# Rotary halves exchanged by DMA, rotation spread over two steps, and routing pieces re-placed in a two-layer attention and expert kernel

## The chip, the cores and the metric

The kernel runs on one core of one Trainium2 chip. The metric is device time of one launch in microseconds (us), as the median of the runs shown. A profile is one further execution, recorded by the hardware profiler; its times are only compared with its own.

The core has five engines which run side by side and meet through semaphores: TensorE (PE in the profile; PEld is its weight load), VectorE (DVE), ScalarE (ACT), GpSimd (POOL) and SyncE (SP), which here only issues DMAs.

## The reference

Input `x` is 16 sequences of 256 tokens with 128 features. Two layers follow each other. A layer normalises `x` and adds an attention and a feed-forward part, both of the normalised `x`. Only the first layer's attention and routing are touched by the change:

```
xn = layernorm(layernorm(x)) * ln_g + ln_b
qk, v = split(xn @ w_qkv.T)                      # queries and keys are the same projection, 8 heads of 64
q = qk*cosq + rotate_half(qk)*sinq               # rotate_half: (x1, x2) -> (-x2, x1), halves of 32
k = qk*cosk + rotate_half(qk)*sink
attn = softmax(q @ k.T, masked to a local window)
out = (attn @ v) @ w_out.T
router: softmax over 8 experts of layernorm(x), the best 2 per token
expert part: gelu MLP of 256 hidden units per expert, weighted; plus one shared MLP
```

The second layer is a gated attention unit and a 32-expert feed-forward part, in which all experts are computed for all tokens. All arithmetic is in float32.

## The kernel before, in words

**Tiling.** The 4096 tokens are eight groups `g` of 512 tokens, two sequences each, laid out with 128 on the partitions. Heads go in pairs, since two heads of 64 fill 128 partitions. So there are 32 head pairs `n = 4*g + hp`; each holds two sequences, and one sequence of one head pair is one *step* `s` of the attention loop: 64 steps, two for each `n`.

**Stages.** The first stage (L485 to L556) runs attention and routing of layer one. The second (L574 on) computes the shared MLP of layer one and then 39 tiles of 256 tokens through their expert. The third (L648 on) gathers the results back and computes layer two.

**What one step does.** The loop `for s in range(-3, NS + 1)` (L500) is a software pipeline written out by hand: `manual_schedule` (L469) keeps the program's order on PE, DVE, ACT and POOL. SP is not in that list. In step `s`:

- PE transposes the probabilities of step `s` (`turned0`, L429, 8 matmuls), computes the scores of step `s+3` (`scores`, L395, 8 matmuls) and the output of step `s-1` (`attended`, L446, 8 matmuls).
- ACT empties the transposes (`evicted`, L436), takes the exponentials of step `s+2` (L411) and copies the output (L451).
- DVE masks the scores of step `s+3` and finds the row maxima (L401), and divides the probabilities of step `s+1` by their sums (`divided`, L417 and L420).

PE's transposes of step `s+1` need the divisions that DVE makes in step `s`.

**The rotation.** `rotated(n)` (L361) is called at the end of every odd step. PE makes two projections, `pq` with `wqk` (L366) and `pw` with `wqks` (L368), whose columns are those of `wqk` with the halves of 32 exchanged. In the next, even, step DVE makes four products (`products`, L377: `pq*cosq`, `pq*cosk`, `pw*sinq`, `pw*sink`) ahead of the scores and of the division, and then two sums (`sums`, L381): that of `q` runs on POOL, that of `k` on DVE after the division. Before the loop the first of these is made at once (L484 to L487).

**Routing.** `routed(g)` (L321) is a generator of eight pieces: moments of the rows (L143 to L149), normalisation (L155 to L166), a transpose, the router's matmuls (L216), the logits, the exponential, the ranking (`before`, five operations of 256 elements on DVE, L200 to L209), and its end. A piece of group `g` runs in step `6*(g-2)+d` for `d` in `(0, 3, 5, 6, 7, 8, 9, 10)` (L477 to L480). `prepare(g)` makes the attention's own input; `values(g, c)` the values (L353).

**Places.** From step 40 on `places0` (L234) works out the row of each token in the list sorted by expert. Its third piece, in step 42, contains the DVE's last partial sums (`ex`, L256) and the PE matmuls over them (L258 to L261). `scatter0(n)` (L308) then writes 128 rows twice by indirect DMA from POOL, in steps 45 to 62. Before that `x_rows` is filled with zeros by one large DMA on SP (L551), in step 10.

Of the kernel before, what the change touches and what calls it, by code (L numbers as in the profile page):

```python
# [11 lines left out]
F32 = mybir.dt.float32  # L12
# [7 lines left out]
P = 128  # L20
# [27 lines left out]
def two_layers(ctx: ExitStack, tc: tile.TileContext, a: dict, out: bass.AP):  # L48
# [17 lines left out]
    def mm_tile(name):  # L66
        tags, n = turn
        turn[1] += 1
        return bank(tags[n % len(tags)], name)
# [4 lines left out]
    def load(name, shape, src=None, eng=None, pool=const):  # L74
        t = pool.tile(shape, F32, tag=name, name=name)
        (eng or nc.scalar).dma_start(out=t, in_=a[name] if src is None else src)
        return t
# [10 lines left out]
    w_a = first.enter_context(tc.tile_pool(name="w_a", bufs=1))  # L88
    wv = load("wv", [P, 512], pool=w_a)
    wqk = load("wqk", [P, 512], pool=w_a)  # L90
    wqks = load("wqks", [P, 512], pool=w_a)
    cosq = load("cosq", [P, N], pool=w_a, eng=nc.sync)
    sinq = load("sinq", [P, N], pool=w_a, eng=nc.sync)
    cosk = load("cosk", [P, N], pool=w_a, eng=nc.sync)
# [141 lines left out]
    def places0(wk):  # L236

        nch = NG * NC
        fl = lambda t: t.rearrange("p n e -> p (n e)")
        top, sel = (wk.tile([P, nch, E0], F32, tag=f"m{i}", name=f"m{i}", bufs=1) for i in range(2))  # L240
        nc.vector.tensor_scalar(fl(sel), fl(rk_all), 2.0, None, ALU.is_lt)
        nc.vector.tensor_scalar(fl(top), fl(rk_all), 0.0, None, ALU.is_equal)
        nc.vector.tensor_tensor(fl(w0_all), fl(sel), fl(pr_all), ALU.mult)
        yield

        acc = sel
        for i in range(5):
            k = 1 << i
            nxt = wk.tile([P, nch, E0], F32, tag=f"cum{i % 2}", name=f"cum{i}", bufs=1)
            nc.vector.tensor_copy(nxt[:, :k, :], acc[:, :k, :])  # L250
            nc.vector.tensor_tensor(nxt[:, k:, :], acc[:, k:, :], acc[:, : nch - k, :], ALU.add)
            acc = nxt
            if i == 2:
                yield
        ex = wk.tile([P, nch, E0], F32, tag="ex", name="ex", bufs=1)
        nc.vector.tensor_tensor(ex, acc, sel, ALU.subtract)  # L256
        pos_ps = mm_tile("pos_ps")[:, : nch * E0]
        nc.tensor.matmul(pos_ps, upper, fl(sel), start=True, stop=False)  # L258
        nc.tensor.matmul(pos_ps, ones, fl(ex), start=False, stop=True)
        cnt = mm_tile("cnt_ps")[:, :E0]  # L260
        nc.tensor.matmul(cnt, ones, acc[:, nch - 1, :], start=True, stop=True)  # L261
        yield
        ns = T // RT
        full = wk.tile([P, E0, ns], F32, tag="full", name="full", bufs=1)
        nc.vector.tensor_tensor(
            full, cnt.unsqueeze(2).to_broadcast([P, E0, ns]), steps.unsqueeze(1).to_broadcast([P, E0, ns]), ALU.is_gt
        )
        used = wk.tile([P, E0], F32, tag="used", name="used", bufs=1)
        nc.vector.tensor_reduce(used, full, AX.X, ALU.add)
        low = wk.tile([P, E0, E0], F32, tag="low", name="low", bufs=1)  # L270
        nc.vector.tensor_tensor(
            low, used.unsqueeze(1).to_broadcast([P, E0, E0]), tie0.rearrange("p (i j) -> p i j", j=E0), ALU.mult
        )
        begin = wk.tile([P, E0], F32, tag="begin", name="begin", bufs=1)
        nc.vector.tensor_reduce(begin, low, AX.X, ALU.add)
        row0 = wk.tile([P, E0], F32, tag="row0", name="row0", bufs=1)
        nc.vector.tensor_scalar(row0, begin, float(RT), None, ALU.mult)
        pos = wk.tile([P, nch, E0], F32, tag="pos", name="pos", bufs=1)
        nc.vector.tensor_tensor(
            pos, pos_ps.rearrange("p (n e) -> p n e", e=E0), row0.unsqueeze(1).to_broadcast([P, nch, E0]), ALU.add  # L280
        )
        yield
        nc.vector.tensor_tensor(fl(sel), fl(sel), fl(top), ALU.subtract)
        for s, m in enumerate((top, sel)):
            at = wk.tile([P, nch, E0], F32, tag="at", name=f"at{s}", bufs=1)
            nc.vector.tensor_tensor(at, m, pos, ALU.mult)
            atr = wk.tile([P, nch], F32, tag="atr", name=f"atr{s}", bufs=1)
            nc.vector.tensor_reduce(atr, at, AX.X, ALU.add)
            nc.vector.tensor_copy(slot_at[:, s, :], atr)
        yield  # L290
        for s, m in enumerate((top, sel)):
            nc.vector.tensor_tensor(m, m, pr_all, ALU.mult)
            nc.vector.tensor_reduce(slot_w[:, s, :], m, AX.X, ALU.add)
        yield

        le = wk.tile([P, NT0, E0], F32, tag="le", name="le", bufs=1)
        nc.vector.tensor_tensor(
            le, begin.unsqueeze(1).to_broadcast([P, NT0, E0]), tiles.unsqueeze(2).to_broadcast([P, NT0, E0]), ALU.is_le
        )
        ex_t = wk.tile([P, NT0], F32, tag="ex_t", name="ex_t", bufs=1)  # L300
        nc.vector.tensor_reduce(ex_t, le, AX.X, ALU.add)
        nc.vector.tensor_scalar(ex_t, ex_t, -1.0, None, ALU.add)
        off = wk.tile([P, NT0], F32, tag="off", name="off", bufs=1)
        nc.vector.tensor_scalar(off, ex_t, float(P), None, ALU.mult)
        nc.vector.tensor_copy(tile_off, off)
        yield
# [15 lines left out]
    with first as pa:  # L322
# [33 lines left out]
        def over(t):  # L356
            return t.unsqueeze(1).to_broadcast([P, 2, N])
# [3 lines left out]
        def rotated(n):  # L361

            g, hp = divmod(n, 4)
            h = slice(hp * P, (hp + 1) * P)
            pq = mm_tile(f"pq_{g}_{hp}")
            nc.tensor.matmul(pq, wqk[:, h], xhTs0[g], start=True, stop=True)  # L366
            pw = mm_tile(f"pw_{g}_{hp}")
            nc.tensor.matmul(pw, wqks[:, h], xhTs0[g], start=True, stop=True)  # L368
            heads[n] = got = [
                wk.tile([P, 2, N], F32, tag=f"rot{what}", name=f"{what}_{g}_{hp}", bufs=3) for what in "qk"  # L370
            ]
            parts = [wk.tile([P, 2, N], F32, tag="rots", name=f"s{what}_{g}_{hp}", bufs=3) for what in "qk"]

            def products():
                for to, ps_, by in ((got, pq, (cosq, cosk)), (parts, pw, (sinq, sink))):
                    for t, m in zip(to, by):
                        nc.vector.tensor_tensor(t, ps_.rearrange("p (b n) -> p b n", n=N), over(m), ALU.mult)  # L377

            def sums():
                for r, part, eng in zip(got, parts, (nc.gpsimd, nc.vector)):  # L380
                    eng.tensor_tensor(r, r, part, ALU.add)  # L381

            turning.append((products, sums))


        def scores(s):
# [78 lines left out]
        with tc.manual_schedule(engines={order.PE, order.DVE, order.Activation, order.Pool}):  # L465
# [13 lines left out]

            pieces = {}  # L480
            for g in range(1, NG):
                for d in (0, 3, 5, 6, 7, 8, 9, 10):
                    pieces.setdefault(6 * (g - 2) + d, []).append(g)

            step(routing, 0, 2)  # L485
            step(preparing, 0, 2)
            rotated(0)  # L487
            products, sums = turning.pop()
            products()
            sums()  # L490
            step(routing, 0, 2)
            step(routing, 1, 2)
            step(preparing, 1)
# [3 lines left out]
            step(routing, 0, 2)  # L497
            step(routing, 1)
            rotated(1)
            for s in range(-3, NS + 1):  # L500
                g, r = divmod(s, 8)
                if 0 <= s < NS:
# [3 lines left out]
                    pTs[s] = evicted(s, tps)  # L506
                if 0 <= s + 2 < NS:
                    sms[s + 2] = exponentials(s + 2, *sc[s + 2])
                products, sums = turning.pop() if turning else (None, None)
                if products:  # L510
                    products()
                    if s + 3 < NS:
                        sc[s + 3] = scores(s + 3)
                    if 0 <= s + 1 < NS:
                        divided(s + 1, sc[s + 1][0], sms.pop(s + 1))
                    sums()
                else:
                    if 0 <= s + 1 < NS:
                        divided(s + 1, sc[s + 1][0], sms.pop(s + 1))
                    if s + 3 < NS:  # L520
                        sc[s + 3] = scores(s + 3)

                if s in (-2, -1):
                    step(routing, 0)
# [5 lines left out]
                    step(preparing, g + 2)  # L530
                if s == 40:
                    placing = places0(wk)
                if 40 <= s < 47:
                    next(placing)
                if s >= 1:
                    attended(s - 1, pTs.pop(s - 1))

                if s % 2 and 2 <= (s + 5) // 2 < NS // 2:
                    rotated((s + 5) // 2)
                if s < 0:  # L540
                    continue
                if r == 2 and g:
# [4 lines left out]
                if s == 10:  # L547
# [1 line left out]
                    nc.gpsimd.memset(zero, 0.0)  # L549
                    x_r0 = x_rows.rearrange("(t p c) d -> p t (c d)", p=P, c=2)  # L550
                    nc.sync.dma_start(out=x_r0, in_=zero.unsqueeze(1).to_broadcast([P, NT0, 2 * D]))  # L551
                if 45 <= s < 63:
                    for n in range((s - 45) * 16 // 9, (s - 44) * 16 // 9):
                        scatter0(n)
            project(NG - 1)
    turn[0] = ["mm", "s", "mm", "o", "mm", "s"]  # L556
# [357 lines left out]
def _laid_out(v):  # L914
# [1 line left out]
    d["x"] = v["L0_attn_x"].reshape(T, D)  # L916
    qk, vv = v["L0_attn_w_qkv"][:512], v["L0_attn_w_qkv"][512:]
    d["wqk"] = qk.T
    d["wqks"] = qk.reshape(HEADS, 2, 32, D)[:, ::-1].reshape(512, D).T
    d["wv"] = vv.T  # L920
    d["wo"] = v["L0_attn_w_out"].T.reshape(4, P, D).transpose(1, 0, 2)
    d["rtw"] = v["L0_ffn_router_w"]
# [57 lines left out]
```

## Time and profile before

| | us |
|---|---|
| three runs | 1104.29, 1105.55, 1106.56 |
| median | 1105.55 |
| profiled execution | 1138.63 |
| its span, first to last instruction | 1136.6 |
| start, up to the output copy of step 0 | 0 to 51.5 |
| copies of steps 0 to 39 (with routing) | 51.5 to 272.5 |
| copies of steps 39 to 45 (with places) | 272.5 to 314.5 |
| copies of steps 45 to 57 (with scatters) | 314.5 to 397.0 |
| copies of steps 57 to 63 | 397.0 to 431.5 |
| second and third stage | 431.5 to 1136.6 |

The stage borders are starts of the copies of the attention output (L451), of which each step has one. In a line of the profile, `out<-in` are tile names of the program, `x128` counts instructions, and the time after `<-` is idle time that ended with the named releaser. The duration of a DVE instruction includes its latency: four divisions of about 350 ns each follow each other every 260 ns, and products of 680 ns every 600 ns. Where several follow on one engine, the spacing is the cost.

### The profile page before, as it was taken

The page shows a single profiled execution, that of the slowest core. Times are in us where ns is not written, and L with a number is a line of the kernel's source. Part 1 is how long each engine was busy: PE and PEld are TensorE (multiplying, and loading weights), DVE is VectorE, ACT ScalarE, POOL GpSimd, SP SyncE. Part 2 cuts the span into 40 slices and gives each one's busy share as a digit, 9 for nine tenths or more (in the row PEclk, how much of TensorE's full clock was granted, in tenths as well). Part 3 has the DMA queues.
Part 4 walks back from the last instruction along what each step waited for, and adds up shares of the span by engine and source line. Part 5 has one row for each costly group of instructions (what it writes and reads, how often), then busy time and mean ns, then how long its engine had stood idle before and what let it go on. Part 6 is the DMA issues. An engine that isn't in the chain of part 4 may idle for free.

```text
span 1136.6 us, 13298 instructions
## 1 busy us (share of the span) xinstructions
PE 983.9 (87%) x3976; PEld 551.0 (48%) x3976; DVE 737.4 (65%) x2346; ACT 442.9 (39%) x1096; POOL 266.0 (23%) x241
## 2 busy tenths in 40 slices
PE   4899899999878859999458797989979699899998
PEld 1455555555444424599433443445444354445453
DVE  3999888989686721233345556667665676758663
ACT  1566666666454643344121222222322223223221
POOL 2111111111156650000243206041240502403020
PEclk9899999999899869999768898999989999899999
DMA  5004100000011115399304242322323323242330
GB/s 157 1 1 142 40 1 1 1 2 1 5 33 38 36 39 164 114 268 265 94 21 116 53 102 56 83 70 73 78 72 84 74 61 83 57 104 56 77 84 9
DMA packets 68471, 80.00 MB, mean 70 GB/s; under 512 B 7976, under 2 KB 43568, under 8 KB 68016
## 3 DMA queue, kind: packets, MB, share of 16 engines
q1 hardware_dynamic: 61984, 69.20, 22.5%
q0 software_dynamic: 4096, 8.40, 2.6%
q10 hardware_dynamic: 2320, 1.56, 0.4%
q8 instruction: 32, 0.52, 0.2%
q14 instruction: 39, 0.32, 0.1%
HBM read 62.09 MB, written 17.04 MB: 70 GB/s over the span
## 4 chain that ended last, share of the span: by engine, by line
PE 62%; DVE 19%; issue 7%; POOL 6%; another core or an unknown queue 2%; DMA 1%; ACT 1%; POOLq 0%; ACTq 0%; DVEq 0%
PE u L853 8%; PE g L851 8%; PE z L862 7%; DVE p L401 4%; PE s L395 4%; POOL yg L668 3%; PE t L429 3%; PE yr L636 3%; PE o L446 3%; PE h L626 3%; DVE p L420 3%; PE o L814 2%; PE pq L366 2%; PE y L457 2%
## 5 line engine op out<-in xcount | busy, mean ns | idle before, releaser
L855 ACT ACTIVATE h<-g 128x512 f32<-128x512 f32 x128 | 76.4, 597 | 268.0 <-PE g L851 267.9
L856 DVE TENSOR_TENSOR h<-h,u 128x512 f32<-128x512 f32 x128 | 87.4, 683 | 82.5 <-PE u L853 81.4
L853 PE MATMUL u<-xn1Ts,eu 128*128 128x512 f32 x256 | 134.6, 614 | 0.0
L851 PE MATMUL g<-xn1Ts,eg 128*128 128x512 f32 x256 | 134.3, 607 | 0.0
L411 ACT ACTIVATE p<-p,nm 128x256 f32<-128x256 f32 x256 | 127.1, 506 | 2.5 <-DVE nm L401 2.5
L401 DVE CUSTOM_DVE_ANT_0 p<-s,mask 128x256 f32<-128x256 f32 x256 | 93.1, 419 | 41.7 <-PE s L395 21.5
L862 PE MATMUL z<-h,ed 128*128 128x512 f32 x224 | 117.5, 607 | 0.0
L668 POOL DMA_INDIRECT yg<-y_rows,slot_at x64 | 67.8, 1059 | 188.5 <-issue 156.1
L429 PE MATMUL t<-ident,p 128*128 128x128 f32 x512 | 74.7, 290 | 33.6 <-DVE p L420 30.0
L436 ACT COPY pT<-t 128x512 f32<-128x512 f32 x128 | 69.4, 589 | 86.1 <-PE t L429 68.0
L789 POOL TENSOR_TENSOR r1s<-r1s,sinr 128x512 f32<-128x512 f32 x16 | 23.2, 1453 | 326.8 <-DVE r1s L787 326.8
L429 PEld LDWEIGHTS t<-ident,p 128*128 128x128 f32 x512 | 62.7, 148 | 70.7 <-issue 44.0
L858 DVE TENSOR_TENSOR h<-h,bc 128x512 f32<-128x512 f32 x128 | 90.8, 710 | 3.0
L395 PE MATMUL s<-k,q 64*128 64x256 f32 x512 | 83.0, 435 | 3.0 <-DVE nm L401 1.1
L446 PE MATMUL o<-pT,v 128*64 128x256 f32 x512 | 74.4, 414 | 11.0 <-ACT oT L451 6.0
L381 POOL TENSOR_TENSOR q<-q,sq 128x512 f32<-128x512 f32 x32 | 40.7, 1272 | 182.2 <-DVE sq L377 182.2
L420 DVE TENSOR_SCALAR p<-p,sm 128x256 f32<-128x256 f32 x256 | 75.9, 359 | 2.3
L853 PEld LDWEIGHTS u<-xn1Ts,eu 128*128 128x128 f32 x256 | 49.5, 198 | 56.9 <-issue 51.2
L851 PEld LDWEIGHTS g<-xn1Ts,eg 128*128 128x128 f32 x256 | 48.0, 196 | 44.2 <-issue 37.7
L862 PEld LDWEIGHTS z<-h,ed 128*128 128x128 f32 x224 | 43.4, 197 | 52.1 <-issue 44.5
L311 POOL DMA_INDIRECT x_rows<-xn_all,slot_at x64 | 62.7, 980 | 22.2 <-issue 17.9
L176 PE MATMUL xn1T<-ident,xn 128*128 128x128 f32 x32 | 10.5, 436 | 61.4 <-DVE xn L155 61.4
(256 smaller groups left out, 1607.6 us busy)
## 6 DMA issues: line engine op xcount, KB each, us to landing
bc<-rows_r SPq DMA_DIRECT2D x128, 256.0 KB, 4.0
we<-in_ex_dram SPq DMA_DIRECT2D x39, 257.0 KB, 4.0
x_rows<-zero SPq DMA_DIRECT2D x1, 4992.0 KB, 16.7
xt<-x_rows SPq DMA_DIRECT2D x39, 128.0 KB, 3.9
y_rows<-yt SPq DMA_DIRECT2D x39, 128.0 KB, 3.5
x<-in_x_dram SPq DMA_DIRECT2D x8, 256.0 KB, 4.6
out_dram<-out SPq DMA_DIRECT2D x8, 256.0 KB, 2.3
x_rows<-xn_all,slot_at POOLq DMA_INDIRECT x64
```

Of the source, the lines that this page charges most:

```text
L395: nc.tensor.matmul(sp[h][:, i, :], q[rows, b, i * P : (i + 1) * P], k[rows, b, :], start=True, stop=True)
L401: nc.vector.tensor_tensor_reduce(out=pr[:, h, i, :], in0=sp[h][:, i, :], in1=mask[:, i, :], scale=-1.0, scalar=-NEG, op0=ALU.add, op1=ALU. ...
L411: nc.scalar.activation(row, row, AF.Exp, bias=nm[:, n : n + 1], scale=-1.0, accum_out=sm[:, n : n + 1])
L420: nc.vector.tensor_scalar(row, row, sm[:, n : n + 1], None, ALU.mult)
L429: nc.tensor.transpose(tp[:, at : at + P], pr[:, h, i, j * P : (j + 1) * P], ident)
L446: nc.tensor.matmul(op[h * DH : (h + 1) * DH, :], vs[g][:, 2 * b + j, (2 * hp + h) * DH : (2 * hp + h + 1) * DH], pT[:, h, j, :], start=(j ...
L668: nc.gpsimd.indirect_dma_start(out=yg[:, 2 * c + s, :], out_offset=None, in_=y_rows, in_offset=bass.IndirectOffsetOnAxis(ap=slot_at[:, s, ...
L851: nc.tensor.matmul(gp, wg, xnT, start=True, stop=True)
L853: nc.tensor.matmul(up, wu, xnT, start=True, stop=True)
L856: nc.vector.tensor_tensor(h, h, up, ALU.mult)
L858: nc.vector.tensor_tensor(h, h, wT[n // 2][:, n % 2, :], ALU.mult)
L862: nc.tensor.matmul(zp, w, r, start=(n == 1), stop=False)
```

## The change

- `wqks` and the projection `pw` are gone. ACT copies `pq` to SBUF (`here`), and four DMAs on SP write it to `there` with each block of 32 partitions exchanged with its neighbour (`q ^ 32`). The copy stands in `later`, so that ACT makes it ahead of its evictions in the next step.
- The rotation takes two steps: `near` (the two cosine products, from PSUM) in the even step, `far` (the two sine products, from `there`) in the odd one after it, followed by both sums on POOL. `rotated` is called one step pair earlier, `(s+7)//2` in place of `(s+5)//2`.
- `divided` comes before `scores` in every step; `near` before both, `far` between them.
- The normalisation of a group moves from `d=3` to `d=2`.
- `places0` has one more `yield`, between `ex` and the matmuls over it. The scatters run in steps 46 to 61, two `n` in each, in place of 45 to 62.

```diff
-    wqks = load("wqks", [P, 512], pool=w_a)
...
         nc.vector.tensor_tensor(ex, acc, sel, ALU.subtract)
+        yield
         pos_ps = mm_tile("pos_ps")[:, : nch * E0]
...
-            pw = mm_tile(f"pw_{g}_{hp}")
-            nc.tensor.matmul(pw, wqks[:, h], xhTs0[g], start=True, stop=True)
             heads[n] = got = [
                 wk.tile([P, 2, N], F32, tag=f"rot{what}", name=f"{what}_{g}_{hp}", bufs=3) for what in "qk"
             ]
-            parts = [wk.tile([P, 2, N], F32, tag="rots", name=f"s{what}_{g}_{hp}", bufs=3) for what in "qk"]
-
-            def products():
-                for to, ps_, by in ((got, pq, (cosq, cosk)), (parts, pw, (sinq, sink))):
-                    for t, m in zip(to, by):
-                        nc.vector.tensor_tensor(t, ps_.rearrange("p (b n) -> p b n", n=N), over(m), ALU.mult)
+            parts = [wk.tile([P, 2, N], F32, tag=f"rots{what}", name=f"s{what}_{g}_{hp}") for what in "qk"]
+            here = wk.tile([P, 2, N], F32, tag="here", name=f"here_{g}_{hp}")
+            there = wk.tile([P, 2, N], F32, tag="there", name=f"there_{g}_{hp}")
+
+            def copied():
+
+                nc.scalar.copy(here.rearrange("p b n -> p (b n)"), pq)
+                for q in range(0, P, 32):
+                    to = q ^ 32
+                    nc.sync.dma_start(out=there[to : to + 32], in_=here[q : q + 32])
+
+            def near():
+                for t, m in zip(got, (cosq, cosk)):
+                    nc.vector.tensor_tensor(t, pq.rearrange("p (b n) -> p b n", n=N), over(m), ALU.mult)
+
+            def far():
+                for t, m in zip(parts, (sinq, sink)):
+                    nc.vector.tensor_tensor(t, there, over(m), ALU.mult)
 
             def sums():
-                for r, part, eng in zip(got, parts, (nc.gpsimd, nc.vector)):
-                    eng.tensor_tensor(r, r, part, ALU.add)
+                for r, part in zip(got, parts):
+                    nc.gpsimd.tensor_tensor(r, r, part, ALU.add)
 
-            turning.append((products, sums))
+            later.append(copied)
+            turning.append([near, far, sums])
...
-                for d in (0, 3, 5, 6, 7, 8, 9, 10):
+                for d in (0, 2, 5, 6, 7, 8, 9, 10):
                     pieces.setdefault(6 * (g - 2) + d, []).append(g)
...
             rotated(0)
-            products, sums = turning.pop()
-            products()
-            sums()
+            drain(later)
+            drain(turning.pop())
...
             rotated(1)
+            drain(later)
+            turning[0].pop(0)()
             for s in range(-3, NS + 1):
...
-                products, sums = turning.pop() if turning else (None, None)
-                if products:
-                    products()
-                    if s + 3 < NS:
-                        sc[s + 3] = scores(s + 3)
-                    if 0 <= s + 1 < NS:
-                        divided(s + 1, sc[s + 1][0], sms.pop(s + 1))
+                if turning and len(turning[0]) == 3:
+                    turning[0].pop(0)()
+                    far = sums = None
+                else:
+                    far, sums = turning.pop(0) if turning else (None, None)
+                if 0 <= s + 1 < NS:
+                    divided(s + 1, sc[s + 1][0], sms.pop(s + 1))
+                if far:
+                    far()
+                if s + 3 < NS:
+                    sc[s + 3] = scores(s + 3)
+                if sums:
                     sums()
-                else:
-                    if 0 <= s + 1 < NS:
-                        divided(s + 1, sc[s + 1][0], sms.pop(s + 1))
-                    if s + 3 < NS:
-                        sc[s + 3] = scores(s + 3)
...
-                if 40 <= s < 47:
+                if 40 <= s < 48:
                     next(placing)
...
-                if s % 2 and 2 <= (s + 5) // 2 < NS // 2:
-                    rotated((s + 5) // 2)
+                if s % 2 and 2 <= (s + 7) // 2 < NS // 2:
+                    rotated((s + 7) // 2)
...
-                if 45 <= s < 63:
-                    for n in range((s - 45) * 16 // 9, (s - 44) * 16 // 9):
+                if 46 <= s < 62:
+                    for n in range(2 * (s - 46), 2 * (s - 45)):
                         scatter0(n)
```

More of the change, by code (lines that the diff above doesn't have):

```diff
@@ L918, in _laid_out @@
     d["wqk"] = qk.T
-    d["wqks"] = qk.reshape(HEADS, 2, 32, D)[:, ::-1].reshape(512, D).T
     d["wv"] = vv.T
```

## The prediction

> **What bounds the kernel now.** First the page, for span and engine shares; second the five stretches of the first stage, since a share over the whole span says nothing of the stage that the change touches; third the waits inside the longest stretch; fourth single durations and the order in time of one stalled step.
>
> ```profile
> span 1136.6 us, 13298 instructions
> ...
> PE 983.9 (87%) x3976; PEld 551.0 (48%) x3976; DVE 737.4 (65%) x2346; ACT 442.9 (39%) x1096; POOL 266.0 (23%) x241
> ```
>
> In the table of stretches the columns are length, PE, PEld, DVE, ACT and POOL busy, granted clock, DMA share and GB/s:
>
> ```profile
> 30.40:51.50 21.10, 18.02 (x82) 10.91 (x81) 20.18 (x83) 11.19 (x39) 3.76 (x3) 0.76 0.01 2
> 51.50:272.50 221.00, 206.48 (x1180) 120.61 (x1180) 200.18 (x777) 150.10 (x471) 36.76 (x32) 0.98 0.07 24
> 272.50:314.50 42.00, 35.72 (x175) 20.16 (x176) 32.11 (x122) 21.72 (x71) 5.48 (x5) 0.88 0.01 4
> 314.50:397.00 82.50, 68.22 (x344) 38.74 (x343) 59.41 (x212) 44.56 (x141) 53.62 (x53) 0.92 0.12 37
> 397.00:431.90 34.90, 21.00 (x112) 11.79 (x111) 8.79 (x37) 14.41 (x44) 15.77 (x17) 0.71 0.10 32
> ```
>
> While routing runs (51.5 to 272.5, 39 steps, 5.67 us each) PE is busy for 93% and DVE for 91%: two engines bound it together, and each now and then waits for the other:
>
> ```profile
> PE t L429 <- DVE p L420: 12.7, 8, 4.0
> DVE p L401 <- PE s L395: 9.0, 15, 1.7
> ```
>
> The eight PE waits come where a step's DVE queue is long: normalisation and ranking both fall in step 6k+3, and the four products of step 6k+4 follow before the division that PE's transposes need. The intervals between output copies show it: 8.92, 9.25, 7.90 and 7.86 us before the copies of steps 16, 22, 28 and 34, among others of 3.6 to 7.1. Step 42 holds the longest wait; PE waits for the partial sums, and then DVE for PE:
>
> ```profile
> 288.10 1.22 PE L259 MATMUL pos_ps<-ex,ones 128*128 128x256 f32 x2 [4.08 <-DVE ex L256]
> ...
> 298.00 0.42 DVE L401 CUSTOM_DVE_ANT_0 p<-s,mask 128x256 f32<-128x256 f32 x1 [8.69 <-PE s L395]
> ```
>
> From step 45 on neither is full (68.2 and 59.4 of 82.5); PE waits 12.3 us there for the division that comes after products and masks.
>
> **What the Trainium skill says.** "DMA: Bandwidth & Descriptors", in the anatomy of one DMA, gives a fixed 2.0 us and bytes over 436 GB/s; for 64 KB that is an estimate of 2.15 us. The trace is near: a 64 KB store from SBUF takes 1.6 us, 64 KB loads 2.2 to 2.6. The same page, on queues, rings and completion order, has descriptors consumed in ring order: a small DMA waits behind a large one of its queue. "SBUF — State Buffer", on the two separate sides, says that a DVE operation with two SBUF inputs and a GpSimd operation that reads SBUF lock each other out for a whole instruction. The trace agrees in the one place where they meet: the first `k` sum, begun while POOL adds `q`, takes 1264 ns instead of 683. "GPSIMD Engine Reference", on elementwise work, has an add on GpSimd 1.96 times as long as on DVE; here it is 1.86:
>
> ```profile
> L381 POOL TENSOR_TENSOR q<-q,sq x32: 1264/1271/1282, 21.4 to 393.4; 128x512 f32<-128x512 f32 x32
> L381 DVE TENSOR_TENSOR k<-k,sk x32: 676/683/1264, 22.0 to 396.8; 128x512 f32<-128x512 f32 x32
> ```
>
> **The change part by part.** *Six steps with routing (three pairs).* Spacings from the order in time on DVE: masks of one step 1.37 us, reciprocal and four divisions 1.26, a product or a sum 0.60. Two steps cost 2 x 2.63 + 4 x 0.60 + 0.60 = 8.26, so six 24.8. One group's routing adds moments 1.3, normalisation 1.5, logits 0.55, ranking 2.7, and `xh` 0.8 x 6/8: together 31.4. The change takes one sum of 0.60 from each pair: 29.6. PE: transposes 0.87, scores 1.06, outputs 1.01 in each step, `pq` and `pw` 1.91 in each pair, and per group values 3.8, projection 3.6, input transpose 0.6 (each x 6/8), router and its transpose 1.6: 17.6 + 5.7 + 6.0 + 1.6 = 31.0, at clock 0.98 31.6; without `pw` 28.1, or 28.7. Before, six steps took 34.0, so the fuller engine was busy for 31.6/34.0 = 0.93. After, DVE is the fuller. I add 0.6 for the port lock: ranking and logits, with two SBUF inputs, follow `far` and its sums in odd steps, and one such meeting costs 1.264 - 0.683 = 0.58. So 30.2/0.93 = 32.5, 1.5 less per six steps, 9.8 us over 39. On top comes what the new order removes of the 12.7 us of PE waits: division ahead of masks, two products in a step instead of four, normalisation away from ranking. I take a third, 4.2. Its bounds are nothing and all. Together **14 us**.
>
> *Exchange.* ACT gains 0.59 us (its 128x512 eviction) in every even step; it is busy for 68% of that stretch and stood idle 48.4 us before its evictions, for the transposes, just where the copy now stands. So it costs nothing; without that cover it would cost 0.59 x 30 = 18 us. On SP nothing but the zero fill stands between 15 and 435 us. Queued issues there follow each other every 0.48 us. The trace has no SBUF-to-SBUF transfer; the nearest rows give
>
> ```profile
> rows_r<-wT SPq DMA_DIRECT2D x8, 64.0 KB, 1.6
> uvs<-in_uvs_dram SPq DMA_DIRECT2D x1, 64.0 KB, 2.6
> ```
>
> and I take 2.2, bounds 1.6 and 4.0 (the usual landing of the 128 to 256 KB rows). The last quarter lands 0.59 + 3 x 0.48 + 2.2 = 4.2 us after `pq` is done. Meanwhile DVE has `near`, a division, masks and the next division before `far`: 1.20 + 1.26 + 1.37 + 1.26 = 5.1 in the lightest steps, 6.9 on average steps. So `far` does not wait; behind it are the masks of its step, for which ACT's exponentials wait.
>
> *Start.* Nothing covers the exchange of `n = 0` and `n = 1`. DVE had `pq` at 19.2 and ended the first products and sum at 23.2; now `far` starts at about 19.2 + 4.2 = 23.4 and ends at 24.6, and the two sums on POOL end near 27.3, ahead of the power operation for group 1 (24.6 to 25.6 before): about 2 us late. `far(1)` stands before the first masks, for which it waits in turn: 32.1 us becomes about 36, and the short step after it may cost 1 more: 5. Against it stands one ACT load less in a row of loads, after which ACT's first activation starts at 14.96; about 1 us. Net **+4**, bounds 0 and +8.
>
> *Zero fill.* Issued at 101.17 in step 10, landing after 16.7, until 117.9. The exchange of step 12, some 11 us later on the same queue, cannot land before about 119, and its `far` is due at 117 to 118.5: **+2**. If the fill goes out ahead of step 10's own exchange it is up to +10.
>
> *Places.* With the extra piece the sums are a step old when PE reaches the matmuls: the 4.08 us go, half of DVE's 8.69 with them: **-4**. The projection (4.6 us there) stays.
>
> *Scatters.* POOL issues one scatter every 1.28 us: 8 in two steps are 10.2, two sums 2.55 and gaps 0.3, so 13.0 us for a pair of steps (6.5 for one). That is more than DVE and PE ask for (5.3 to 5.5), so POOL sets the pace between the sums of steps 47 and 57: five pairs, 65 us, and 2.7 for the last sums until the scores of step 59 may start. Those 12 steps took 82.5 - 5.7 = 76.8 (5.7 is a DVE wait that the profile gives to no engine); I take 72 with the entry and exit of that chain, **-5**, bounds -9 and +3. The scatters end about 98 us after step 46 begins, near 410; the tiles that read them start near 475, behind the shared MLP.
>
> Sum: -14 + 4 + 2 - 4 - 5 = -17. The profiled execution, 1138.6 for a span of 1136.6, would become 1121.6. It stands 33 us above the median of the runs, and 22 us of its chain are waits given to no engine, between 347 and 421, which I cannot assign; so I carry the difference over: 1105.6 - 17 = **1088.6**.
>
> **Rivals.** *Exchange late (slower).* If a quarter takes 4.0 us to land, like the larger rows, the last lands after 6.0, and DVE waits up to 0.9 in light steps, more where the four run one after the other; PE and ACT then wait behind the masks. At 1 us for each of 30 pairs it is 1088.6 + 30 = **1118**. It decides from 17/30 = 0.57 us per pair. For it: no row shows such a transfer; against it: all 64 KB rows are under 2.7 us. *Port lock (same).* POOL's 2.55 us of sums meet DVE operations in every pair, not once in six steps: 0.58 x 30 = 17 us, **1106**. For it: the 1264 ns; against it: masks and `near` read PSUM, and come first after `far`. *GpSimd bound early (smaller gain).* Scatters and sums gain nothing over 76.8 us, and the order recovers none of the PE waits: 1088.6 + 5 + 4 = **1098**. That the exchange does not replace the second projection is not possible; that its absence is hidden is, since DVE and PE are both full: that is the low end of the 14.
>
> **Numbers.** The forecast, with its own range of 1077 to 1096, has 0.45; the smaller gain (1096 to 1103) 0.20; the port lock 0.10, half of it within 0.2%; late exchange 0.22; a larger gain (all PE waits gone, under 1077) 0.03. A measurement of this kernel tells 0.2%, 2.2 us, from no change. Faster: 0.45 + 0.20 + 0.03 + 0.02 = 0.70; same 0.06; slower 0.24. The range reaches from 1076 into the late case, to 1113.
>
> **What would show it.** Right: no `pw` row; about 5.3 us between output copies up to step 39, without the intervals above 7.8; no DVE wait on a DMA at the `there` products after step 14; the wait before L259 gone; POOL full between the sums of steps 47 and 57. Wrong: DVE idle before the `there` products in every pair, with a landing above 3 us; divisions or rankings stretched beside POOL's sums; or PE idle before scores, released by POOL, already in the first 40 steps.

## The result, and the profile after

The changed kernel takes 1094.12 us (median of 4 runs, 1092.04 to 1097.65), the kernel before 1106.05 (4 runs, 1104.29 to 1106.70). The ratio is 0.9898, with a 95% interval of 0.9869 to 0.9926: 11.9 us faster, where 17 were forecast.

One thing has to be known for all that follows: chips differ. On two of the chips of the experiments the kernel before takes about 1106 us, on two others about 1139, and the difference lies in the stretch with the scatters. (Each chip was measured in one session, so chip and session can't be told apart.) The profiled execution of the kernel before that the prediction reads (1138.6) was of the second kind; the profile of the changed kernel is of the first. The kernel before was therefore profiled once more (first experiment below), and the comparisons here use that profile unless another is named.

From the page of the changed kernel, span and busy times:

```profile
span 1090.3 us, 13540 instructions
...
PE 956.3 (88%) x3912; PEld 538.9 (49%) x3912; DVE 737.0 (68%) x2314; ACT 460.0 (42%) x1128; POOL 316.4 (29%) x273
```

The same five stretches of the changed kernel, cut at the copies of steps 0, 39, 45, 57 and 63 (columns as in the prediction):

```profile
30.40:58.10 27.70, 20.59 (x86) 13.14 (x87) 21.56 (x88) 13.32 (x44) 7.86 (x6) 0.69 0.13 30
58.10:266.00 207.90, 196.87 (x1139) 116.08 (x1137) 192.58 (x764) 161.09 (x491) 69.06 (x53) 0.98 0.19 51
266.00:300.40 34.40, 32.23 (x169) 18.54 (x170) 31.33 (x118) 23.22 (x73) 9.14 (x7) 0.90 0.10 22
300.40:370.20 69.80, 57.34 (x323) 32.88 (x322) 64.54 (x207) 47.42 (x148) 53.83 (x52) 0.95 0.21 60
370.20:390.10 19.90, 17.86 (x119) 10.54 (x118) 8.34 (x38) 13.60 (x43) 15.74 (x17) 1.00 0.14 44
```

Routing and places are shorter, the start is longer. The stretch with the scatters is the odd one: PE is busy for 57.3 of 69.8 us only, DVE for 64.5, though the routing is over.

### The profile page after: what moved, and what is told of

Same layout as the page of the kernel before. It is cut to its first block, busy times and chain, and to the rows that moved or that the text cites. A ratio compares the mean times of both kernels' runs of the same rounds, so it can differ in the third digit from the quotient of the medians.

```text
span 1090.3 us, 13540 instructions
## 1 busy us (share of the span) xinstructions
PE 956.3 (88%) x3912; PEld 538.9 (49%) x3912; DVE 737.0 (68%) x2314; ACT 460.0 (42%) x1128; POOL 316.4 (29%) x273
## 4 chain that ended last, share of the span: by engine, by line
PE 58%; DVE 20%; issue 9%; POOL 7%; DMA 3%; ACT 1%; SPq 1%; POOLq 0%; ACTq 0%; DVEq 0%
PE u L865 8%; PE g L863 8%; PE z L874 7%; DVE p L412 4%; DVE p L431 3%; PE s L406 3%; POOL yg L680 3%; PE yr L648 3%; PE h L638 3%; PE o L457 3%; PE o L826 3%; PE y L468 2%; PE pq L366 2%; PE t L440 2%; PE y L599 1%
## 5 line engine op out<-in xcount | busy, mean ns | idle before, releaser
L406 PE MATMUL s<-k,q 64*128 64x256 f32 x512 | 90.3, 425 | 25.3 <-DVE nm L412 15.3
L391 POOL TENSOR_TENSOR q<-q,sq 128x512 f32<-128x512 f32 x32 | 49.4, 1542 | 134.8 <-DVE sq L387 110.6
L431 DVE TENSOR_SCALAR p<-p,sm 128x256 f32<-128x256 f32 x256 | 81.5, 382 | 2.3
L440 PEld LDWEIGHTS t<-ident,p 128*128 128x128 f32 x512 | 60.3, 143 | 43.8 <-issue 12.7
L406 PEld LDWEIGHTS s<-k,q 64*128 64x128 f32 x512 | 53.9, 196 | 48.7 <-DVE nm L412 22.6
L440 PE MATMUL t<-ident,p 128*128 128x128 f32 x512 | 70.4, 280 | 7.9 <-DVE p L431 7.2
```

Of the source, the lines that this page charges most:

```text
L406: nc.tensor.matmul(sp[h][:, i, :], q[rows, b, i * P : (i + 1) * P], k[rows, b, :], start=True, stop=True)
L431: nc.vector.tensor_scalar(row, row, sm[:, n : n + 1], None, ALU.mult)
L440: nc.tensor.transpose(tp[:, at : at + P], pr[:, h, i, j * P : (j + 1) * P], ident)
```

## The experiments

In each, the changed kernel's profile is the one above; times are compared with runs of the kernel before on the same chip.

**1. The kernel before, once more.** No edit.

> The kernel before, profiled once more. If the 33 us by which its first profiled execution exceeded the runs belong to that execution alone, the time is near 1105, the waits given to no engine between the copies of steps 45 and 63 are gone, and that stretch takes 85 to 95 us in place of 117. If they belong to the kernel, the span is again near 1136 and those waits are there again.

It took 1105.61 us. The table of stretches of that execution:

```profile
30.40:52.60 22.20, 19.06 (x83) 11.13 (x83) 21.13 (x87) 11.82 (x40) 3.76 (x3) 0.77 0.01 1
52.60:273.60 221.00, 206.52 (x1180) 120.69 (x1180) 200.24 (x777) 150.10 (x470) 36.73 (x32) 0.98 0.07 24
273.60:315.50 41.90, 35.59 (x175) 20.09 (x176) 32.07 (x122) 21.68 (x70) 5.51 (x5) 0.88 0.01 4
315.50:382.00 66.50, 60.96 (x338) 34.46 (x337) 57.90 (x207) 44.33 (x142) 50.93 (x50) 0.97 0.14 44
382.00:400.20 18.20, 17.96 (x119) 10.41 (x117) 11.65 (x43) 13.44 (x43) 14.27 (x15) 1.00 0.15 48
```

The first three stretches are those of the first profile to within 1.2 us. The fourth takes 66.5 in place of 82.5 us and the fifth 18.2 in place of 34.5 (34.9 with the last 0.4), so the extra 33 us are not the kernel's own. So the account of the change, after minus before, is:

| | before | after | difference | forecast |
|---|---|---|---|---|
| start, to the copy of step 0 | 52.6 | 58.1 | +5.5 | +4 |
| routing, steps 0 to 39 | 221.0 | 207.9 | -13.1 | -14, +2 for the zero fill |
| places, 39 to 45 | 41.9 | 34.4 | -7.5 | -4 |
| scatters, 45 to 57 | 66.5 | 69.8 | +3.3 | -5 |
| end of the loop, 57 to 63 | 18.2 | 19.9 | +1.7 | none |
| the rest | 703.4 | 700.2 | -3.2 | none |
| span | 1103.6 | 1090.3 | -13.3 | -17 |

The rest holds the same instructions in both; over the eight kernels with the change that were profiled on such chips it is 700.1 to 704.5, so its 3.2 are not told from chance.

The other rows have their scatter too. In four kernels which are the same up to step 39 (the changed one and those of experiments 3, 4 and 6), the copies of steps 0 to 17 take 94.3, 97.7, 94.2 and 95.6 us, those of steps 17 to 39 113.6 in all four. So the routing stretch of one profile is good to some 4 us, and where less is at stake only steps 17 to 39, called the steady part below, are compared.

**2. The start without the exchange.**

```diff
+    wqks = load("wqks", [P, 256], pool=w_a)
...
+            if n < 2:
+                pw = mm_tile(f"pw_{g}_{hp}")
+                nc.tensor.matmul(pw, wqks[:, h], xhTs0[g], start=True, stop=True)
+                there = pw.rearrange("p (b n) -> p b n", n=N)
...
-            later.append(copied)
+            if n >= 2:
+                later.append(copied)
```

> The changed kernel, but head pairs 0 and 1 take their exchanged halves from a second projection, as before, and make no exchange by DMA. Theory (uncovered exchange at the start): the copy of step 0 moves from 58.1 back to about 52 and the time falls by 5 to 7 us, to 1087 to 1089. Rival (the start is late for another reason, such as both sums on GpSimd ahead of the power operation, or clock): less than 2 us, 1092 to 1094.

1088.98 us; ratio to before 0.9834 (0.9813 to 0.9855). The copy of step 0 is at 51.5 again. The uncovered exchange is the cost of the start, and it is 5 to 7 us (5.1 between the medians, 6.6 at the copy of step 0). In the order of time of the changed kernel it reads so (first products of the exchanged halves for `n = 0`, the same for `n = 1`, then the first masks, which were at 33.18 before):

```profile
24.59 0.69 DVE L387 TENSOR_TENSOR sq<-there,sinq 128x512 f32<-128x512 f32 x1 [2.63 <-DMA there<-here]
...
38.75 0.69 DVE L387 TENSOR_TENSOR sq<-there,sinq 128x512 f32<-128x512 f32 x1 [2.69 <-DMA there<-here]
...
39.96 0.42 DVE L412 CUSTOM_DVE_ANT_0 p<-s,mask 128x256 f32<-128x256 f32 x1
```

DVE waits twice for the DMA, 5.3 us in all, and the masks are 6.8 us late; ACT's copy for `n = 1` stood behind an exponential of the router, itself late by DVE's first wait.

**3. Both sums of the late head pairs on VectorE.**

```diff
-                for r, part in zip(got, parts):
-                    nc.gpsimd.tensor_tensor(r, r, part, ALU.add)
+                engs = (nc.vector, nc.vector) if n >= 26 else (nc.gpsimd, nc.gpsimd)
+                for r, part, eng in zip(got, parts, engs):
+                    eng.tensor_tensor(r, r, part, ALU.add)
```

> The changed kernel, with both sums of head pairs 26 to 31 on VectorE, those which meet the scatters on GpSimd. Theory (GpSimd's queue and its lock of the shared port hold up the scatter stretch): the divisions of 506 ns mean there return to 350, PE's waits for the k sum vanish, the copies of steps 45 to 57 take 62 to 65 us in place of 69.8, and the time falls by 4 to 8 us. Rival (that stretch is bound by PE and ScalarE anyway): VectorE's added 7 us show, and the time stays within 2 us or rises.

1082.69 us; ratio 0.9782 (0.9766 to 0.9799), 11.4 us under the changed kernel's median; of the two profiled executions, the last copy of this one is 6.9 us earlier (383.2 against 390.1). The copies of steps 45 to 57 take 62.9 us in place of 69.8, as the theory had it; the time fell by more than the 4 to 8 us expected. What had held them up is in the changed kernel's groups and waits between 300.4 and 370 us:

```profile
L431 DVE TENSOR_SCALAR p<-p,sm 128x256 f32<-128x256 f32 x52 | 23.1, 506 | 0.5
...
L387 DVE TENSOR_TENSOR sk<-there,sink 128x512 f32<-128x512 f32 x6 | 6.8, 1131 | 0.0
```

```profile
PE s L406 <- POOL k L391: 8.4, 3, 4.1
```

A division takes 506 ns there on average, against 349 in the routing stretch and 394 in the same stretch of the kernel before; the product `sk` takes 1131 against 684. The order in time shows one case:

```profile
359.68 4.47 DVE L431 TENSOR_SCALAR p<-p,sm 128x256 f32<-128x256 f32 x4
360.38 1.27 POOL L391 TENSOR_TENSOR q<-q,sq 128x512 f32<-128x512 f32 x1
361.61 1.26 POOL L391 TENSOR_TENSOR k<-k,sk 128x512 f32<-128x512 f32 x1
362.92 0.73 PEld L406 LDWEIGHTS s<-k,q 64*128 64x128 f32 x8 [4.29 <-POOL k L391]
362.92 1.26 PE L406 MATMUL s<-k,q 64*128 64x256 f32 x8 [4.06 <-POOL k L391]
363.03 1.00 POOL L311 DMA_INDIRECT x_rows<-xn_all,slot_at  x1 [0.17 <-issue]
```

POOL reaches the two sums late, since eight scatters stand ahead of them. They then fall on DVE's divisions instead of its masks: four divisions take 4.47 us in place of 1.14 (the routing stretch), PE waits 4.06 us for the `k` sum, and `far` of the next pair comes late too. With the sums on DVE the divisions of the same stretch are at 379:

```profile
L432 DVE TENSOR_SCALAR p<-p,sm 128x256 f32<-128x256 f32 x48 | 15.3, 379 | 0.4
```

**4. Half of the scatters left out.**

```diff
-        for s in range(2):
+        for s in range(1):
             ins = nc.gpsimd.indirect_dma_start(
```

> The changed kernel without the scatters of each token's second expert, so that half of the scatters and those rows are left out. Theory (scatters and sums fill GpSimd and set the pace from step 47 to 59): the copies of steps 45 to 57 take 61 to 64 us in place of 69.8 and the time falls by 6 to 9 us. Rival (GpSimd is hidden): within 2 us.

(This kernel leaves out the rows of each token's second expert.) 1081.32 us; ratio 0.9768 (0.9751 to 0.9785), 12.8 us under the changed kernel's median, where 6 to 9 were expected. The stretch takes 59.4 us, and the divisions in it 395 ns. Fewer scatters and no sums on GpSimd are two ways to relieve the same engine, and they bring the stretch to 59.4 and 62.9 us: the theory holds, the rival, that GpSimd is hidden, falls. Neither experiment parts the two ways in which GpSimd did harm, PE's waits for a late `k` sum and DVE operations held while a sum runs, since both go together.

**5. Normalisation back beside the ranking.**

```diff
-                for d in (0, 2, 5, 6, 7, 8, 9, 10):
+                for d in (0, 3, 5, 6, 7, 8, 9, 10):
```

> The changed kernel with the normalisation piece put back from d=2 to d=3, into the step of the ranking. Theory (the prediction's: the stall that both together caused is a third of what the order gains): the copies of steps 0 to 39 take 3 to 6 us more than 208, with one interval in six above 8 us again. Rival (division ahead of everything hides the long step by itself): within 1 us.

1096.74 us; ratio 0.9909 (0.9892 to 0.9925), not told apart from the change's 0.9898. From the copy of step 17 to that of step 39 it takes 113.6 us, as the changed kernel does; of the intervals there only two differ, those before the copies of steps 33 and 34 (4.47 and 8.47 in place of 5.33 and 7.61), and their sum is the same. The 3.9 us that its routing stretch is longer lie before step 17, where equal kernels differ by as much, and 3.0 of them in a longer wait behind the zero fill (5.4 us against 2.4). So the placing of this piece is worth nothing in the steady part. The theory that it was a third of the order's gain falls.

**6. The places without their pause.**

```diff
-        yield
         pos_ps = mm_tile("pos_ps")[:, : nch * E0]
...
-                if 40 <= s < 48:
+                if 40 <= s < 47:
```

> The changed kernel without the added pause in the places, so that the matmuls over the sums stand in step 42 again. Theory (the pause alone shortens the places): the copies of steps 39 to 45 take 38.5 to 42 us in place of 34.4, with a PE wait of about 4 us before L259. Rival (most of the 7.5 us there came from the new order): under 2 us more.

1100.25 us; ratio 0.9944 (0.9925 to 0.9962). The copies of steps 39 to 45 take 40.8 us in place of 34.4; the order in time has the wait again:

```profile
281.49 0.42 DVE L255 TENSOR_TENSOR ex<-cum,m 128x256 f32<-128x256 f32 x1
...
281.96 1.22 PE L258 MATMUL pos_ps<-ex,ones 128*128 128x256 f32 x2 [5.73 <-DVE ex L255]
```

So nearly all of the 7.5 us belongs to one `yield`.

**7. A second projection that nobody reads.**

```diff
             nc.tensor.matmul(pq, wqk[:, h], xhTs0[g], start=True, stop=True)
+            pw = mm_tile(f"pw_{g}_{hp}")
+            nc.tensor.matmul(pw, wqk[:, h], xhTs0[g], start=True, stop=True)
```

> The changed kernel with a second projection computed for each head pair and not read, so that PE has the old load and all else is as changed. Theory (PE and DVE bound the routing stretch together, DVE now the fuller): PE asks for 5.25 us a step and becomes the bound; the copies of steps 0 to 39 take 5 to 11 us more than 208. Rival (the gain there is all DVE's and the order's): under 2 us more.

1111.35 us; ratio 1.0054 (1.0037 to 1.0071). The routing stretch takes 224.7 us, 16.8 more. One half of that is not PE's: in this kernel SP issues the zero fill ahead of the exchange of step 10, and DVE waits for it:

```profile
DVE sq L389 <- DMA there<-here: 10.8, 1, 10.8
```

In the changed kernel the fill comes one exchange later and the wait is 2.4 us. That is 8.4 of the 16.8; the other 8.4 are within the 5 to 11 expected. The steady part gives PE's share more cleanly: 116.6 us against 113.6, and against 125.0 in the kernel before. PE's old load costs 3.0 of the 11.4 us that the change gains there.

**8. Both repairs together** (the edits of 2 and 3).

> The changed kernel with the second projection for head pairs 0 and 1 and both sums of head pairs 26 to 31 on VectorE. If the two losses are apart from each other: 1094 - 5.5 - 12 = 1076 to 1078. If one hides the other: 1080 to 1083.

1080.01 us (1076.60 to 1083.10); ratio 0.9758 (0.9730 to 0.9787). It has the lowest median of the kernels with the whole computation, 26.3 us under the kernel before, though its interval overlaps that of experiment 3. Its runs cover both what was expected if the two losses are apart (1076 to 1078) and the 1080 of the case that one hides the other; its routing stretch takes 211.9 us in place of 207.9, with the same 113.6 in the steady part.

The next two kernels were measured on a chip on which the kernel before takes 1138.88 us (20 runs). Their stretches up to the scatters can be compared with the others, since the kernel before has the same intervals there on both kinds of chip.

**9. The order alone, in the kernel before.**

```diff
-                    products()
-                    if s + 3 < NS:
-                        sc[s + 3] = scores(s + 3)
                     if 0 <= s + 1 < NS:
                         divided(s + 1, sc[s + 1][0], sms.pop(s + 1))
+                    products()
+                    if s + 3 < NS:
+                        sc[s + 3] = scores(s + 3)
                     sums()
```

> The kernel before, with the division ahead of the products and masks in every step, and nothing else of the change. Theory (dropped projection 8 us of the routing stretch, the order most of the other 5): the PE waits for the division, 12.8 us there, fall to 4 or less, the copies of steps 0 to 39 take 215 to 218 us in place of 221, and the time falls by 3 to 8 us. Rival (the order only moves the wait to the scores, and it is the sum moved to GpSimd that gave the other 5): 220 to 222 us there, and the time within 2 us.

1142.81 us; ratio 1.0038 (1.0024 to 1.0052), so it is slightly slower as a whole, with 90.0 us in the scatter stretch of that chip against 82.5 in the first profile. The routing stretch takes 218.6 us, 2.3 less. The PE waits for the division have gone, but others took their place; in its list of waits of that stretch:

```profile
DVE p L401 <- PE s L395: 12.4, 12, 3.0
PE s L395 <- DVE sm L417: 10.5, 7, 3.9
```

The 218.6 us lie between what the theory and the rival say, but in mechanism the rival is nearer: with four products in one step, the wait moves from the transposes to the scores. (Its second half, that the `k` sum moved to GpSimd gave the rest, fails in the next experiment.)

**10. The k sum on VectorE everywhere** (the edit of 3 with `(nc.gpsimd, nc.vector)` for all `n`).

> The changed kernel with the k sum on VectorE in all head pairs, as before the change, so that GpSimd has one sum. Theory: routing stretch within 3 us of 208, as PE and not VectorE bounds it after the dropped projection as before; scatter stretch 63 to 67 in place of 69.8, since GpSimd has 1.27 us less in each pair and holds the port for one sum instead of two; time 1087 to 1092. Rival (the prediction's: VectorE is the fuller engine of the routing stretch): 3 to 12 us more there.

1131.59 us; ratio 0.9940 (0.9918 to 0.9963), so on that chip too a kernel with the rest of the change is faster than before. Routing takes 211.8 us, 3.8 more than the changed kernel; in the steady part it is 114.7 against 113.6, with DVE busy for 110.3 us in place of 106.8. The absolute times that were expected don't apply on that chip, nor does its scatter stretch (84.1 us) compare.

**11. The zero fill ahead of the loop, on top of both repairs.**

```diff
+            zero = w_a.tile([P, 2 * D], F32, tag="zero", name="zero")
+            nc.gpsimd.memset(zero, 0.0)
+            x_r0 = x_rows.rearrange("(t p c) d -> p t (c d)", p=P, c=2)
+            nc.sync.dma_start(out=x_r0, in_=zero.unsqueeze(1).to_broadcast([P, NT0, 2 * D]))
             step(routing, 0, 2)
```

(The same lines go from step 10.)

> The changed kernel with the second projection for head pairs 0 and 1, both sums of head pairs 26 to 31 on VectorE, and the zero fill of x_rows issued ahead of the loop instead of in step 10, where exchanges queue behind it. Against the kernel with the first two edits alone (1080.0): 2 to 4 us less, 1076 to 1078, and no DVE wait on the exchange after the start. Rival (the wait behind the fill is made up for within the next steps): 1079 to 1081.

> The kernel with both edits and the earlier zero fill once more, since in the call before the kernel before itself took 1138.9 us instead of 1106 on the chip of that call. Theory (the stop of 74 us in step 47 belongs to that chip's scatters, not to the edit): where the kernel before takes about 1106, the copies of steps 45 to 57 take 62 to 65 us and the time is 1075 to 1080. Rival (scatters that follow each other without a sum between them, and the earlier fill, stop the other engines anywhere): more than 1090 again.

Run twice, on two chips, both with the kernel before at 1139: 1146.62 us, ratio 1.0071 (1.0050 to 1.0093), and 1147.37, ratio 1.0084 (1.0069 to 1.0100). The waits of DVE for the exchange are gone and routing takes 210.1 and 209.0 us, but from the copy of step 46 to that of step 47 it takes 74 us, both times, with few instructions on PE, ACT and DVE in between, while GpSimd goes on with its scatters. From the order in time of the first, DVE's longest pause, a scatter, and PE behind DVE:

```profile
344.39 0.42 DVE L420 CUSTOM_DVE_ANT_0 p<-s,mask 128x256 f32<-128x256 f32 x1 [33.97 <-issue]
344.79 0.97 POOL L312 DMA_INDIRECT x_rows<-xn_all,slot_at  x1 [0.30 <-issue]
345.22 1.22 PE L414 MATMUL s<-k,q 64*128 64x256 f32 x2 [15.18 <-DVE nm L420]
```

DVE's pause has no releaser that the profile knows, and so it is with ACT's and one of PE's in that stretch. The cause is open, and so is what the kernel takes on a chip of the other kind, and whether the two repairs gain on these chips.

## Why the prediction was right or wrong, point by point

**Direction, and size to within 6 us: right.** The routing stretch, the largest term, became shorter by 13.1 us where 14 less 2 were forecast. That the sum came so near is partly luck: between the two profiles the scatters and the end of the loop are 10.0 us off one way, and places, routing and the rest 7.8 the other.

**The working of the 14: right sum, wrong shares.** I gave 9.8 to the lower demand of the fuller engine and 4.2 to the order. The steady part of the kernel before, of experiment 7 (PE's old load put back) and of the changed kernel:

```profile
148.60:273.60 125.00, 118.69 (x668) 68.23 (x668) 112.15 (x436) 85.53 (x267) 19.74 (x17) 0.99 0.00 1
166.60:283.20 116.60, 116.42 (x673) 68.29 (x673) 107.30 (x426) 91.38 (x279) 38.07 (x28) 1.00 0.11 26
152.40:266.00 113.60, 110.33 (x646) 65.23 (x646) 106.78 (x425) 91.11 (x278) 37.71 (x28) 1.00 0.12 27
```

With PE's load put back, 8.4 of the 11.4 us gained remain, and PE is busy all but 0.2 us, where it had been idle for 6.3. The k sum is worth 1.1, the piece's place nothing, and the order alone, with four products in a step, 2.1. What is left, about 5 us, none of these has by itself. That it is the division of the products over two steps together with the order is what remains by elimination; it was not tried alone, nor was the dropped projection without the rest. The step that failed here is "the same share of time busy": PE's share was 0.95 and became 0.97, or 1.00 with its load put back. Nor did DVE become the fuller engine: it is busy for 106.8 us to PE's 110.3, and 3.5 us more of work on it cost 1.1 (experiment 10). The long intervals before the copies of steps 16, 22, 28 and 34 (8.92, 9.25, 7.90, 7.86) became 5.54, 7.45, 6.78 and 7.61; the working had passed over a fifth of 7.87, before step 10, which is 7.62 now.

The 0.6 for the port lock came as forecast, on the router's small operations with two SBUF inputs. The divisions take 349 ns as before, but this product after the exponential is held in most groups (changed kernel, then the kernel before):

```profile
L229 DVE TENSOR_TENSOR pr_all<-pr_all,rsm x8: 191/686/704, 44.7 to 262.6; 128x32 f32<-128x32 f32 x8
L230 DVE TENSOR_TENSOR pr_all<-pr_all,rsm x8: 191/192/193, 37.7 to 268.8; 128x32 f32<-128x32 f32 x8
```

Together with a subtraction on the logits, 0.68 in place of 0.19 us in four groups, it is some 0.7 us for each group; with one sum on GpSimd (experiment 10) both are at 0.19 again. POOL waits too: its `q` sum takes 1583 ns on average in place of 1273 in the routing stretch, behind the `sk` product. The lock of the Trainium skill ("SBUF — State Buffer", who interferes with whom) works both ways, the operation issued first holding the other off, and I had priced one way.

**Exchange: right.** A quarter lands in 2.0 us, where 2.2 was taken; the late exchange did not come. From the uses of `there` in the changed kernel:

```profile
L379 SPq DMA_DIRECT2D there<-here x128: 507/584/1508, 20.7 to 357.4; - x128
...
  DMA there<-here: 7.7, 3
...
DMA to landing us min/median/max: 1.9/2.0/6.4
```

DVE waits three times in the whole run: for `n = 0`, for `n = 1`, and once behind the zero fill. That last wait is 2.4 us, forecast 2; and the 10 us named for the case that the fill goes first were met by experiment 7 (10.8). The issues follow each other every 0.63 us, where 0.48 was taken. The 2.15 us that I worked out from "DMA: Bandwidth & Descriptors" (anatomy of one DMA) is near the 2.0, but that section of the Trainium skill describes DMAs issued from GpSimd, and these are issued on SP.

**Start: right mechanism, a little more.** 5.5 us for 4; the copy for `n = 1` queued behind a late exponential, which I had not followed.

**Places: right mechanism, mis-sized.** 7.5 for 4. I took half of DVE's 8.69 us wait to be hidden by the projection; experiment 6 shows 6.4 us for the pause alone.

**Scatters: wrong in sign.** "-5, bounds -9 and +3" became +3.3, and 1.7 more behind it. What failed is the base. The 76.8 us were those of a chip on which engines stop for nothing that the profile names; I took out one such wait of 5.7 us, but on the chips of the runs the stretch is 66.5. The 72 us forecast for the stretch after the change are near the 69.8 measured, and POOL's pace was right (13.0 us for a pair; the sums of the changed kernel follow each other every 12.6 to 13.1). What I left out of that pace is its lock: late sums fall on divisions and cost DVE up to 3.3 us a pair (4.47 - 1.14). The same page of the Trainium skill (who interferes with whom) names two kinds of VectorE operation that can be locked out: those with two SBUF inputs, and those in a 2-port mode. I had quoted only the first, to which the stretched `sk` belongs. A division has one tensor and a scalar per row as inputs; that it is the second kind is how I read its stretching, and no run here shows the mode itself. Experiments 3 and 4 show the place: without GpSimd's load there, 7 to 10 us come back in this stretch.

**Carrying the 33 us over to the runs** was right for the sum: the runs did not have them. But they could not be left in the base of the scatters as well.

## What to carry to other kernels

Work moved to an idle engine has to be followed into the stretch where that engine is not idle: the `k` sum on GpSimd gained 1.1 us in the steady part, but the two sums cost some 7 us in the 12 steps with scatters, where they came late, kept PE waiting and fell on VectorE's divisions. A software pipeline hides a DMA of 2 us in all steps but those in which it has not started; give those the old way. And make sure that the profile read and the times to be predicted come from the same kind of chip: a stretch with waits that no releaser explains is the first to be doubted.

## What the runs showed of the hardware

- SBUF to SBUF, 32 partitions of 2 KB each, issued on SP: landing after 1.9 to 2.0 us (median), issues of 0.58 us each, 0.63 from start to start; behind a 4992 KB fill on the same queue up to 16.2 us.
- A scatter of 128 rows of 512 B keeps GpSimd for 1.28 us when they follow each other, on both kinds of chip.
- On the chips on which the kernel before takes 1139 us, PE, ACT and DVE stop during the scatters: the copies of steps 45 to 63 take 117 us in the kernel before in place of 85, and one step takes 74 us in experiment 11, where 64 scatters follow each other without sums between them; the landing of a scatter is 3.7 to 3.9 us there (median), against 2.2 to 2.3.
- A router product of two SBUF inputs on VectorE takes 0.69 us in place of 0.19 where it falls on the second of two sums on GpSimd.
